# Order edges in a two-block model kernel, and a different end for its output projection

## The chip, the cores and the metric

The kernel runs on one core of one Trainium2 chip. The metric is the device time of one execution in microseconds (us). Three runs of the kernel before gave a median of 1876.63 us (1872.15 to 1878.21).

## What is computed

Four sequences of 256 tokens with 512 features (1024 tokens in all, float32) go through two blocks. Each step is x = x + f(layernorm(x)):

```python
x = x + L0_attn(ln(x))   # linear attention with a memory: sig_q @ M / (sig_q @ z), output projection
x = x + L0_ffn(ln(x))    # base matmul plus top-2 of 8 low-rank experts
x = x + L1_attn(ln(x))   # the mixer, below
x = x + L1_ffn(ln(x))    # base matmul plus top-1 of 4 low-rank experts
```

The mixer is a state-space layer. Its input projection gives, per token, a gate and x (8192 channels each), B and C (8 groups of 128 each) and dt (128 heads):

```python
x, B, C = silu(conv4(proj))                  # causal convolution over 4 tokens
dt = softplus(dt + dt_bias); A_dt = -exp(A_log) * dt
Y = (C B^T * exp(segsum(A_dt))) @ (x * dt) + (carry from the chunk before) + D * x
y = Y * rsqrt(mean(Y^2) + eps) * norm_w * silu(gate)
return y @ out_proj_w.T                      # 8192 -> 512
```

## The kernel before

The program is written once in order, and a scheduler then orders the instructions of every engine. It takes the written order as priority and its own estimates of time as readiness, so an instruction that looks ready can be placed ahead of one written earlier. Each engine then runs its own queue strictly in that order, and waits for semaphores where data or buffers come from another engine. `with tc.issue_after(ins):` adds an edge: each instruction of the block that runs on the same engine as `ins` is queued somewhere behind `ins`. It fixes no more than that, and it affects no other engine. The kernel keeps the instructions that edges refer to in `last`.

**First block (lines 198 to 350).** Eight token tiles of 128 are normalized (`layernorm`, L103 to L123: statistics on DVE, sqrt on ACT, `xn` on ACT or DVE, four transposes on PE, a copy to `xnT` on ACT). Eight heads follow in a pipeline (`queries`, `retrieve`, `turn`), then the output projection with weights `wo`, which POOL sums from four parts (L236 to L238), then the expert layer (`lora_mixture`, L146).

**Mixer (L353 to L992).** `time_steps` (L404) computes dt on all heads. It loads A_log and takes its exponential on ACT (L412). Then 72 units are worked through: 8 groups, each of one `bc` unit (its B and C channels) and 8 `pair` units (128 channels, that is two heads). A pair's unit has these stages:

- `stage_a` (L607) projects 1024 tokens to 256 channels (x and gate) with seven products of half-size blocks in place of eight (Strassen's scheme; token sums `tok`, weight sums `wsum` by POOL, L511 to L514). `project` (L517) issues them in four steps: each `product` is two 128x512 matmuls into PSUM banks `pd`, `pa`, `pb`; `keep` (L537, ACT) saves an intermediate value, and DVE adds at L549, L553 and L556 combine them. The instruction at L553 is `last["one"]`, the one at L556 `last["two"]`; the bank `pa` is used again by PE after L556 has read it. The weights of unit n+2 are loaded at the end of unit n.
- `stage_t` (L640), one unit later: transposes of xT (L683, into the only `mm2` bank pair), xdt and xdr (DVE, L686, L693), and the decay masks `cst`: loaded, 16 Relu (L705) and one Exp (L709) on ACT, multiplied with the group's `gt` on DVE (L711).
- `stage_c` (L716), two units later: 24 small matmuls `ps_y` (L725, L733), then on DVE y = D*x + ps_y (L741), on ACT the square (L743), on DVE y * norm_w * silu(gate) (L744) and the running sum of squares (L747).

The output projection is worked in as channel tiles become ready. Two tiles form one block i, and again seven products replace eight, for each half m of the 512 outputs. A product with number p covers two blocks (i-1, i) for one m; it is a PSUM bank `mm1` (two of them) that ACT copies to SBUF (L809) and POOL adds to `prod_d` in DRAM (L811). `begin_out` makes the token sums (L777) and queues seven products; a unit issues two of them after its first step and the rest after its third. POOL makes the weight sums (`out_weight_sums`, L763). Blocks 0 to 30 are done this way; channel tiles 62 and 63 are multiplied directly at the end.

**Order by hand.** In units 0 to 4 the dictionary `early` (L891) gives the stages that `turn` (L899) issues behind the last PE instruction, and `last["bar"]` holds all later products of `project` behind them. From unit 5 on `last["bar"]` is None. `last["pe"]` is the PE instruction written last.

**End.** Two further rounds of the loop (n = 72, 73) finish stages and products: block 30's fourteen products are added by DVE (L830) to what `load_prods` (L817) has loaded from `prod_d`. `put_together` (L832) combines seven products to four parts on DVE, for m = 0 and 1. The sum over channels for the norm is made by eight one-column matmuls (`ps_var`, L972). `finish(t)` (L979) puts two direct products and four transposed parts in one bank per token tile, adds to x (L992) and normalizes; the last expert layer follows, interleaved by `ready`.

Of the kernel before, what the change touches and what calls it, by code (L numbers as in the profile page):

```python
# [33 lines left out]
P = 128  # L34
# [19 lines left out]
def model_kernel(ctx: ExitStack, tc: tile.TileContext, a: dict, out: bass.AP):  # L54
# [25 lines left out]

    def toks(t):
        return slice(t * P, (t + 1) * P)
# [20 lines left out]
    def layernorm(t, psum, xnp, on_act=False):  # L103
# [19 lines left out]
        nc.scalar.copy(xnT[:, :, toks(t)], ps.rearrange("p (k t) -> p k t", k=KT))  # L123
# [74 lines left out]
    with ExitStack() as c0:  # L198
# [31 lines left out]
        for h in range(NKV):  # L230
# [7 lines left out]
            nc.gpsimd.tensor_tensor(wo[:, h, :], wo[:, h, :], s[:, 3, :], ALU.add)  # L238
# [114 lines left out]
    with ExitStack() as c1:  # L353
# [12 lines left out]
        last = {"pe": None, "one": None, "two": None, "adt": None, "bar": None}  # L366
# [37 lines left out]
        def time_steps():  # L404
# [7 lines left out]
            nc.scalar.activation(na, na, AF.Exp)  # L412
# [104 lines left out]
        def project(n, one, two):  # L517
# [17 lines left out]
            def keep(ps, i):  # L535
                c = snp.tile([P, 512], F32, tag=f"keep{i}", name=f"keep{n}_{i}")
                nc.scalar.copy(c, ps)  # L537
                return c
# [175 lines left out]
        ys = []  # L714

        def stage_c(n):  # L716
# [5 lines left out]
            for c in range(NT):  # L722
# [21 lines left out]
            nc.vector.scalar_tensor_tensor(  # L744
                y, y, normw[:, j : j + 1], hd["sg"], ALU.mult, ALU.mult
            )
            nc.vector.tensor_tensor(ssq, ssq, sq, ALU.add)  # L747
# [12 lines left out]

        osums, ysums = {}, {}

        def out_weight_sums(i):  # L763
            if 2 * i + 2 < NPAIR:
# [34 lines left out]
        def out_product(m, p, over, bank, to):  # L799

            ps = Psum.tile([P, 512], F32, bank, f"ps_p{over[-1]}_{m}_{p}")
# [3 lines left out]
            to(ps, m, p, over)  # L805

        def add_up(ps, m, p, over):
            st = osp.tile([P, 512], F32, tag="prod", name=f"prod{over[-1]}_{m}_{p}")
            nc.scalar.copy(st, ps)  # L809
            first = over[0] == 0  # L810
            nc.gpsimd.dma_start(  # L811
                out=prod_d[m][p // 2][p % 2], in_=st, accum_op=ALU.bypass if first else ALU.add
            )

        prods = []

        def load_prods():  # L817
            homes = [bcp.tile([P, 2, 512], F32, tag=f"tok{q}", name=f"out_a{q}") for q in range(3)]
            homes += [wsp.tile([P, 2, 512], F32, tag="wsum", name=f"out_b{q}") for q in range(2)]
            homes += [b2.tile([P, 2, 512], F32, tag="raw", name=f"out_c{q}") for q in range(2)]  # L820
            rest = homes[6]
            for m in range(2):
                tiles = homes[3 * m : 3 * m + 3]
                for q in range(3):
                    nc.sync.dma_start(out=tiles[q], in_=prod_d[m][q].rearrange("c p t -> p c t"))
                nc.sync.dma_start(out=rest[:, m], in_=prod_d[m][3][0])
                prods.append([tiles[p // 2][:, p % 2] for p in range(6)] + [rest[:, m]])

        def add_last(ps, m, p, over):
            nc.vector.tensor_tensor(prods[m][p], ps, prods[m][p], ALU.add)  # L830

        def put_together(m):  # L832

            g = prods[m]
            op = nc.vector.tensor_tensor
# [18 lines left out]
        def out_products(n, bank, to):  # L854
            for _ in range(min(n, len(todo))):
                m, p, over = todo.popleft()
                out_product(m, p, over, bank, to)
# [10 lines left out]
        next(steps)  # L868
        token_sums()
        for j in range(6):  # L870
            load_wout(j)
        for i in range(3):
            out_weight_sums(i)
# [14 lines left out]
        def first_sums(_):  # L888
# [7 lines left out]
            4: ([(stage_t, 2)], [(stage_c, 1)], [(stage_c, 2), (stage_t, 3)]),  # L896
        }

        def turn(n, i):  # L899

            if n not in early:
                step, m = [(None, 0), (stage_c, n - 2), (stage_t, n - 1)][i]
                if step and 0 <= m < len(units):
                    step(m)
# [7 lines left out]
        for n in range(len(units) + 2):  # L912
            a_steps = stage_a(n) if n < len(units) else iter(())
            bank, to = ("mm1", add_up) if n < len(units) else ("in", add_last)
            if n == len(units):
                load_prods()
# [147 lines left out]
```

## Time and profile before

| what | value |
|---|---|
| median of three runs | 1876.63 us |
| the profiled execution | 1876.13 us |
| its span in the profile | 1874.4 us |
| PE busy | 1804.8 us (96%) |
| DVE busy | 1366.1 us (73%) |
| ACT busy | 1166.4 us (62%) |
| POOL busy | 695.4 us (37%) |
| mean granted TensorE clock | 0.986 |
| mean DMA | 128 GB/s |

PE is TensorE's matmuls, PEld its weight loads, DVE the vector, ACT the scalar and POOL the GpSimd engine; SP issues DMAs. A share of busy time is an average over stages with different limits, so the views by stage and the waits of one engine say more than this table. A float32 matmul of 128x512 appears as two instructions in the trace and takes 0.857 us in all. The last instruction of the trace is the add at L194 of the last token tile and the store behind it.

### The profile page before, as it was taken

Reading aid. Unit: us, or ns where it says so; the run is one execution under the profiler, and the core shown is the slowest. Engines: PE = TensorE matmul, PEld = TensorE weight load, DVE = VectorE, ACT = ScalarE, POOL = GpSimd, SP = SyncE. Lnnn points to the kernel's source line nnn. Section 1 sums busy time; section 2 is a strip of 40 time slices with the busy share of each in tenths; the row PEclk is TensorE's granted clock in tenths of the full one; section 3 lists DMA queues with packets and bytes.
Section 4 is the critical chain, followed back from the end, with each engine's and each line's share of the span. In section 5 each row is a group of like instructions: output and inputs, shape, how many; then the busy total and the mean of one; then the engine's idle time right before and its main releaser. Section 6 shows DMA issues by size and latency. Waiting matters only on the chain.

```text
span 1874.4 us, 21313 instructions
## 1 busy us (share of the span) xinstructions
PE 1804.8 (96%) x7666; PEld 945.0 (50%) x7666; DVE 1366.1 (73%) x1495; ACT 1166.4 (62%) x2059; POOL 695.4 (37%) x681
## 2 busy tenths in 40 slices
PE   7999897999999999999999999999999999999988
PEld 4545544554554555455545454455454545455564
DVE  4433597888687868786878677887786887778871
ACT  3321238877577748775777676758775767766620
POOL 6311241335344533454235533543444344533100
PEclk9999998999999999999999999999999999999989
DMA  8100123345555555654555545554655555456701
GB/s 313 61 0 6 53 95 118 141 148 134 141 141 140 141 140 140 149 145 107 158 140 145 131 119 140 152 138 133 144 139 117 160 144 152 107 134 156 218 23 45
DMA packets 80329, 239.20 MB, mean 128 GB/s; under 512 B 9472, under 2 KB 10496, under 8 KB 70880
## 3 DMA queue, kind: packets, MB, share of 16 engines
q1 hardware_dynamic: 48768, 171.49, 25.8%
q0 software_dynamic: 30880, 65.30, 21.5%
q8 instruction: 61, 1.00, 0.2%
q10 hardware_dynamic: 576, 1.05, 0.2%
q14 instruction: 44, 0.36, 0.1%
HBM read 177.78 MB, written 60.03 MB: 127 GB/s over the span
## 4 chain that ended last, share of the span: by engine, by line
PE 63%; ACT 14%; DVE 14%; DMA 5%; issue 4%; POOL 0%; SPq 0%; DVEq 0%; ACTq 0%; POOLq 0%
PE pa L526 17%; PE ps_p L804 12%; PE pd L526 8%; ACT cst L709 4%; ACT cst L705 4%; PE ps_y L725 4%; PE pb L526 4%; DMA cst<-cs_d 4%; PE f_pso L172 3%; PE ps_o L307 3%; PE ps_q L95 3%; DVE xT L569 3%; DVE cst L711 2%; PE ps_xt L683 2%; PE ps_y L733 2%
## 5 line engine op out<-in xcount | busy, mean ns | idle before, releaser
L811 POOL DMA_DIRECT2D prod_d<-prod x210 | 178.0, 927 | 524.8 <-ACT prod L809 509.9
L705 ACT ACTIVATE cst<-cst,cs 128x128 f32<-128x128 f32 x1024 | 326.7, 395 | 31.4 <-DMA cst<-cs_d 31.0
L711 DVE TENSOR_TENSOR cst<-cst,gt 128x1536 f32<-128x1536 f32 x128 | 232.7, 1842 | 113.9 <-ACT cst L709 113.8
L569 DVE SCALAR_TENSOR_TENSOR xT<-raw,convw,xT 128x1020 f32<-128x1020 f32 (+2 forms) x216 | 300.9, 1394 | 1.6
L511 POOL TENSOR_TENSOR wsum<-win 128x256 f32<-128x256 f32 x72 | 94.1, 1307 | 354.5 <-DMA win<-in_win 198.7
L743 ACT ACTIVATE xdt<-xT 128x1024 f32<-128x1024 f32 x64 | 67.7, 1058 | 253.1 <-DVE xT L741 253.1
L709 ACT ACTIVATE cst<-cst 128x3072 f32<-128x3072 f32 x64 | 176.9, 2764 | 0.7
L804 PE MATMUL ps_p<-xT,wout 128*128 128x512 f32 x372 | 172.2, 595 | 1.4 <-DVE xT L744 1.4
L725 PE MATMUL ps_y<-cst,xdt 128*64 128x128 f32 x2048 | 161.1, 276 | 0.1
L526 PE MATMUL pa<-xnT,wsum 128*128 128x512 f32 x288 | 144.6, 625 | 9.0 <-ACT keep L537 8.9
L526 PE MATMUL pa<-tok,win 128*128 128x512 f32 x288 | 137.4, 600 | 12.2 <-DVE sg L556 12.1
L725 PEld LDWEIGHTS ps_y<-cst,xdt 128*64 128x64 f32 x2048 | 120.0, 137 | 52.7 <-issue 49.2
L526 PE MATMUL pd<-tok,wsum 128*128 128x512 f32 x288 | 139.0, 604 | 6.5 <-POOL wsum L511 4.5
L526 PE MATMUL pa<-xnT,win 128*128 128x512 f32 x288 | 136.8, 596 | 0.0
L526 PE MATMUL pa<-tok,wsum 128*128 128x512 f32 x288 | 135.8, 593 | 0.8 <-ACT keep L537 0.8
L549 DVE TENSOR_TENSOR raw<-pb,keep 128x512 f32<-128x512 f32 x72 | 49.4, 686 | 118.4 <-PE pb L526 118.1
L526 PE MATMUL pd<-xnT,wsum 128*128 128x512 f32 x288 | 135.6, 592 | 0.1
L526 PE MATMUL pb<-xnT,win 128*128 128x512 f32 x288 | 135.6, 592 | 0.0
L809 ACT COPY prod<-ps_p 128x512 f32<-128x512 f32 x210 | 117.7, 575 | 25.6 <-PE ps_p L804 21.3
L804 PEld LDWEIGHTS ps_p<-xT,wout 128*128 128x128 f32 x372 | 70.0, 190 | 88.2 <-issue 84.3
L804 PE MATMUL ps_p<-ysum,osum 128*128 128x512 f32 x248 | 112.1, 593 | 0.0
L537 ACT COPY keep<-pa 128x512 f32<-128x512 f32 x144 | 83.0, 577 | 38.6 <-PE pa L526 38.5
(217 smaller groups left out, 3178.3 us busy)
## 6 DMA issues: line engine op xcount, KB each, us to landing
cst<-cs_d SPq DMA_DIRECT2D x64, 1536.0 KB, 6.3
prod_d<-prod POOLq DMA_DIRECT2D x210, 256.0 KB, 4.3
win<-in_win SPq DMA_DIRECT2D x144, 256.0 KB, 3.9
wout<-in_wout SPq DMA_DIRECT2D x64, 256.0 KB, 4.1
wo_s<-in_wo POOLq DMA_DIRECT2D x8, 1024.0 KB, 5.9
wq<-in_wq SPq DMA_DIRECT2D x8, 256.0 KB, 3.7
x_d<-x SPq DMA_DIRECT2D x8, 256.0 KB, 2.0
xr<-x_d SPq DMA_DIRECT2D x2, 1024.0 KB, 7.4
```

What stands on the lines that cost most here:

```text
L511: op(v[:, 0], w[:, 1, 0:2], w[:, 1, 2:4], ALU.add)
L526: last["pe"] = nc.tensor.matmul(ps, lhsT=wt[:, k, :], rhs=tk[:, k, :], start=start and k == 0, stop=k == 1, skip_group_check=not start,)
L537: nc.scalar.copy(c, ps)
L569: nc.vector.scalar_tensor_tensor(d[:, :, k:], src[:, :, : SEQ - k], convw[:, i, TAPS - 1 - k : TAPS - k], d[:, :, k:], ALU.mult, ALU.add,)
L705: nc.scalar.activation(m[:, hh, c, :], m[:, hh, c, :], AF.Relu, bias=cs[:, c, h : h + 1], scale=1.0)
L709: nc.scalar.activation(mf, mf, AF.Exp, scale=-1.0)
L711: nc.vector.tensor_tensor(mf[:, hh], mf[:, hh], gr.rearrange("p c l -> p (c l)"), ALU.mult)
L725: last["pe"] = nc.tensor.matmul(flat(py)[e, toks(c)], lhsT=xdt[:, c, e], rhs=m[:, hh, c, :], start=True, stop=c % 2 == 0,)
L743: nc.scalar.activation(sq, y, AF.Square)
L804: last["pe"] = nc.tensor.matmul(ps, lhsT=w, rhs=y, start=i == over[0], stop=i == over[-1])
L809: nc.scalar.copy(st, ps)
L811: nc.gpsimd.dma_start(out=prod_d[m][p // 2][p % 2], in_=st, accum_op=ALU.bypass if first else ALU.add)
```

## The change

It has these parts:

1. The exponential of A_log is queued behind the last copy to `xnT` on ACT (`marks["xnT"]`), and the first three weight sums of the output projection behind the last sum of `wo` on POOL (`marks["wo"]`). Unit 0's products are queued behind the matmuls of dt on PE.
2. `early` gets entries for units 5 and 6, so that `last["bar"]` stays in force up to unit 6.
3. The last two DVE instructions of `stage_c` become `stage_d`, queued on DVE behind `last["two"]`. The ACT copies of the products of a unit's first step are queued behind the unit's last `keep`; the copies of its third step come after all its products (`add_up` works off the list `taken`).
4. Seven-product blocks end at block 29 (`SEVEN` is 30). The last four channel tiles (60 to 63) are multiplied directly, eight token tiles times four. Four token tiles begin early: with tiles 60 and 61 before the last `stage_c`, with tile 62 behind it. The loop has no rounds 72 and 73; the last seven products of block 29 (m = 0) go through DRAM like the others and are loaded again by `load_prods(0)`. `put_together(1)` runs on POOL, `put_together(0)` on DVE.

```diff
-        nc.scalar.copy(xnT[:, :, toks(t)], ps.rearrange("p (k t) -> p k t", k=KT))
+        marks["xnT"] = nc.scalar.copy(xnT[:, :, toks(t)], ps.rearrange("p (k t) -> p k t", k=KT))
...
-            nc.scalar.activation(na, na, AF.Exp)
+            with issue_after(marks["xnT"]):
+                nc.scalar.activation(na, na, AF.Exp)
...
-            nc.vector.scalar_tensor_tensor(
-                y, y, normw[:, j : j + 1], hd["sg"], ALU.mult, ALU.mult
-            )
-            nc.vector.tensor_tensor(ssq, ssq, sq, ALU.add)
+            outputs[n] = y, sq, hd["sg"]
+
+        def stage_d(n):
+            if n not in outputs:
+                return
+            j, (y, sq, sg) = units[n][1], outputs.pop(n)
+            with issue_after(last["two"]):
+                nc.vector.scalar_tensor_tensor(y, y, normw[:, j : j + 1], sg, ALU.mult, ALU.mult)
+                nc.vector.tensor_tensor(ssq, ssq, sq, ALU.add)
             ys.append(y)
...
         next(steps)
+        last["bar"] = last["pe"]
         token_sums()
         for j in range(6):
             load_wout(j)
-        for i in range(3):
-            out_weight_sums(i)
+        with issue_after(marks["wo"]):
+            for i in range(3):
+                out_weight_sums(i)
...
-            4: ([(stage_t, 2)], [(stage_c, 1)], [(stage_c, 2), (stage_t, 3)]),
+            4: ([(stage_t, 2)], [(stage_c, 1), (stage_d, 1)], [(stage_c, 2), (stage_d, 2), (stage_t, 3)]),
+            5: ([], [(stage_c, 3)], [(stage_d, 3), (stage_t, 4)]),
+            6: ([], [(stage_c, 4)], [(stage_d, 4), (stage_t, 5)]),
...
-            out_products(2, bank, to)
+            next(a_steps)
+            out_products(2)
             turn(n, 0)
-            next(a_steps, None)
+            next(a_steps)
+            with issue_after(last["keep"]):
+                add_up()
             turn(n, 1)
-            next(a_steps, None)
-            out_products(share - 2, bank, to)
+            next(a_steps)
+            out_products(share - 2)
+            add_up()
...
+        last["two"] = None
+        load_prods(1)
+        for p in ORDER:
+            out_product(0, p, (SEVEN - 1,))
+            add_up()
+        N = len(units)
+        with issue_after(last["pe"]):
+            stage_c(N - 2)
+            stage_d(N - 2)
+            stage_t(N - 1)
+        load_prods(0)
...
+        parts = {1: put_together(1)}
+        AHEAD = 4
+        with issue_after(last["pe"]):
+            for t in range(AHEAD):
+                for j in (NPAIR - 4, NPAIR - 3):
+                    out_project(t, j, "mm1" if t < 2 else "in")
+        with issue_after(last["pe"]):
+            stage_c(N - 1)
+            stage_d(N - 1)
+        with issue_after(last["pe"]):
+            for t in range(AHEAD):
+                out_project(t, NPAIR - 2)
+        pv = Psum.tile([P, 2, 512], F32, "mm2", "ps_var")
+        with issue_after(last["pe"]):
+            for t in range(NT):
+                last["pe"] = nc.tensor.matmul(
+                    pv[:, 0, t : t + 1], lhsT=ssq[:, toks(t)], rhs=ones, start=True, stop=True
+                )
...
+        parts[0] = put_together(0)
...
-            for j in (NPAIR - 2, NPAIR - 1):
-                nc.tensor.matmul(
-                    ps, lhsT=ys[j][:, toks(t)], rhs=wouts[j], start=j == NPAIR - 2, stop=j == NPAIR - 1
-                )
+            for j in [NPAIR - 1] if t < AHEAD else range(NPAIR - 4, NPAIR):
+                with issue_after(last["pe"]):
+                    out_project(t, j)
+            ps = outs.pop(t)
```

## The prediction

> **What bounds the kernel now.** The busy times by stage come first: each row is a stretch of the span, then the busy time of PE, PEld, DVE, ACT and POOL, the granted TensorE clock, and the DMA.
>
> ```profile
> 0.00:215.00 215.00, 192.69 (x696) 105.99 (x696) 92.41 (x250) 56.00 (x93) 59.17 (x67) 0.98 0.26 93
> 215.00:360.00 145.00, 130.97 (x536) 69.12 (x537) 120.30 (x109) 89.87 (x152) 43.07 (x40) 0.93 0.29 105
> 360.00:1760.00 1400.00, 1378.77 (x5993) 709.58 (x5992) 1092.06 (x1020) 992.32 (x1768) 591.10 (x574) 1.00 0.55 140
> 1760.00:1875.00 115.00, 102.39 (x444) 60.32 (x442) 61.31 (x119) 28.19 (x48) 2.09 (x3) 0.92 0.22 63
> ```
>
> PE is the bound everywhere: 1804.8 of 1874.4 us. An order of issue can only win PE's idle time (22, 14, 21 and 13 us in the four stages) and the work done at a low clock. So I list the waits of PE, then its timeline at the longest ones; the bracket is the idle time before an instruction and what ended it.
>
> ```profile
> 22.80 1.12 PE L122 MATMUL ln_ps<-ident,xn 128*128 128x128 f32 x4 [4.54 <-ACT xn L117]
> ...
> 328.16 3.75 PE L526 MATMUL pd<-tok,wsum 128*128 128x512 f32 x4 [3.70 <-POOL wsum L511]
> ...
> 574.46 1.98 PE L526 MATMUL pa<-tok,win 128*128 128x512 f32 x4 [1.34 <-DVE sg L556]
> ...
> 1791.14 3.58 PE L972 MATMUL ps_var<-ones,ssq 128*128 128x1 f32 x16 [4.92 <-DVE ssq L747]
> ```
>
> Within 360 to 1760 the list of waits has three entries only: DVE sg L556 9.3 us in 8 times, ACT keep L537 8.9 us in 8, DVE xT L741 2.9 us in 5.
>
> **First block.** ACT's timeline shows why PE stood at 22.8:
>
> ```profile
> 21.73 0.31 ACT L412 ACTIVATE per_head<-per_head 128x128 f32<-128x128 f32 x1 [5.17 <-DMA per_head<-in_A_log]
> 21.95 0.80 ACT L117 ACTIVATE xn<-x,ln_sh,ln_rs 128x512 f32<-128x512 f32 x1
> ```
>
> The Exp of A_log waits for its load, and the last token tile's xn stands behind it. The edge sends the Exp behind the last xnT copy (214.3), where ACT is idle for 12.24 us and where the result is not read until L450 at 252.3. Won: 4.54 us, and the clock, granted at 0.64 from 22.8 to 30.0 (7.2 x 0.36 = 2.6): 7.1. What is late next: the tile's shift is ready at 16.26; xn 0.81, transposes 0.44 and copy 0.57 end at 18.1, just where PE stopped (18.3). Added: the table load of 1.28 that hid in this wait now stands before head 0's first Exp; ps_n of that head waited only 0.27, so between 0 and 1.28 shows, and I take 0.6, since ps_q of the next head covers some. On POOL the osum sums of two blocks (8 x 0.72) go behind the last wo sum (66 us); their reader is at 317, and POOL has nothing then until 111.8: nothing. Net -6.5 (bounds -3 and -7.1, the weak end if the later wq loads fall behind).
>
> **First seven units.** At 328.16 unit 6's first product stood in PE's queue before unit 5's rest; its weights could be loaded only when unit 4's last product ended (322), so 3.70 and, before it, 1.39 us were idle, and about 2.3 us went to a clock of 0.74 and 0.53 over 322 to 332. Edges for units 5 and 6 forbid that order: -7.4. They also forbid what filled 309 to 315: unit 5's pa, pb and pa, while stage_c(2) waited for the masks' products L711 (313.3). PE will stand there: L711 can end between 311.1 (the Exp's end at 307.6 plus 2 x 1.75) and 313.3, so 2.0 to 4.2, and L741 adds 1.3 before the transposes: 3.3 to 5.5, with 0 to 3.4 of cold clock. ps_dt before unit 0's first product (215.66, run in 1.8 us before wdt was used) is between -0.3 and +1. Net between -4.4 and +2.5; I take -2.5, nearer the gain because the longest wait in the trace is the one removed.
>
> **Each pair.** The DVE queue at 574:
>
> ```profile
> 571.38 1.28 DVE L744 SCALAR_TENSOR_TENSOR xT<-xT,normw,sg 128x1024 f32<-128x1024 f32 x1
> 572.58 1.22 DVE L747 TENSOR_TENSOR ssq<-ssq,xdt 128x1024 f32<-128x1024 f32 x1
> 573.72 0.68 DVE L556 TENSOR_TENSOR sg<-pa,keep 128x512 f32<-128x512 f32 x1
> ```
>
> L744 and L747 are stage_d; the edge puts them behind L556. L556 then ends at 572.0, before PE is through with pd (573.1): the 1.34 goes, and no other wait takes its place. That is 9.3 us over 8 places; I take 8.5. Where no wait shows (L556 at 377.96, L744 at 380.23) the order is this already. Readers of y come later by 0.68 us; the next product is 3.4 us further on.
>
> The 210 copies L809 (0.57 each) go behind keep. Cover: at 394.70 keep ends, two copies end at 395.8, and the product that wants their bank starts at 398.11, 2.3 us later. In the 8 places where keep is late (2.08 us at 636.4), two copies stood ahead of it, 1.1 us; but there a product already ran in front (633.18), which now waits for the copies. So between 0 and 1.1 a place is won; I take 1.5 in all. POOL's writes of prod move with the copies by up to 5 us; behind them stand the weight sums, due a unit (21 us) later, and the osum sums: nothing. If that cover is gone it is the second rival. Net -10 (bounds -14 and, without the rival, 0).
>
> **Tail.** Removed: the 4.92 before ps_var, and the cold clock after it, 0.50 over 1791.1 to 1798 and 0.81 to 1802 (3.4 + 0.8): 9.1. Now four products with channel tile 62 (4 x 0.857 = 3.43) lie over the chain L741, L744, L747 (3.6); 0.3 stays, 1.5 if two other DVE adds get in between as now; I take 0.7: -8.4. Products: 21 closing ones become 7, 16 direct ones become 32: two more, +1.7. The part transposes are the same.
>
> New wait: the last unit's transposes (ps_xt) follow stage_c of the unit before at once, and all eight direct products stand behind them by an edge. In the trace 8.8 us of products lay between (1766.87 to 1775.65). PE will be there at 1760.5 + 7 x 0.857 + 2.75 = 1769.3. They need L741 (1.28) and the Silu of the last xT, which ended at 1771.0 on an ACT without a gap since 1757.5, and ACT now gets seven copies (4.0) that DVE did as L830. So 1.7 to 5.7; I take 3, since DVE loses fourteen L830 and four L777 and the conv ends earlier. The price of such a wait at the clock: the Trainium skill (TensorE: Matmul & The Clock Gate, HAM oscillation) says idle gaps above about 3.4 us make the clock fall. The rows put it lower: after 2.81 us (269.3) the clock was 0.66 over the next 5 us, after 2.85 us (1828.4) 0.59 over 7, after 2.08 and 1.34 it stayed 1.00. By the rule my 3 us cost nothing more; by the rows up to 3.4. I follow the rows at half, 1.7: +4.7.
>
> The products' return through DRAM: last one 1766.5, copy 0.6, issue 0.9, landing 4.4, load 4.6, seven DVE adds 4.2: 1781.7, against a first use near 1788. Cover 6 us, also for the loads queued on SP in front. put_together(1) on POOL: seven adds of 128x512 at 1.27 (row L236) from 1769 to 1778, due at 1788. Here the skill speaks against the change (SBUF — State Buffer, Who interferes with whom): a DVE operation with two SBUF inputs and a GpSimd one exclude each other, the later blocks whole; that would be up to 7 x 1.27 = 8.9 us of DVE. The row: L777 took 0.68 alone and 1.21 beside POOL sums (558.13), 0.53 more, so 3.7 for seven. I take the row; on PE's path it is inside the 3 us above. By the rule the tail would end 4 later. Unchanged: the last layernorm's wait of 2.85 and its cold clock, 2.9. Net -2 (bounds -6 and +4).
>
> **Sum.** -6.5 - 2.5 - 10 - 2 = -21. The profiled execution took 1876.13 us (span 1874.4, 1.7 around it): 1855.1. It lies 0.5 under the median of the three runs, 1876.63, so 1855.5.
>
> **Rivals.** (a) The edges of the units do not do what they say: an edge fixes a place on one engine, and the rest of the order is chosen anew, so that the small waits of units and tail come back elsewhere and only the A_log fix counts: 1876.6 - 6.5 = 1870. For it: 21 us of idle time in 72 units is already little, and the remaining waits have three different releasers. Against it: L556's eight waits have one cause each time. Its low variant, in which only the tail pays back, lies near 1864.
> (b) Slower: copies behind keep starve the two product banks. Place: the third product of a unit. It decides when the copies end over 2.3 us after keep, that is, when ACT puts a table load and an Exp (1.28 + 2.76 = 4.0) between. The first bank is then free at 394.7 + 4.0 + 0.6 = 399.3, 1.2 us after 398.11; in half of the 60 units with products that is 36 us, and 1855 + 36 = 1891. For it: the Exp follows keep closely, at 370.9 and 373.4. Against it: there the product starts at 377.09, after the Exp's end at 376.1 plus a copy.
> (c) Nothing: the stall at 309 gets its cold clock, the tail takes its bad end (+2.5, +4), the pairs give nothing: 1876.6 - 6.5 + 6.5 = 1877.
>
> **How the numbers follow.** Forecast 0.54 (1840 to 1865), (a) 0.20, (b) 0.17, (c) 0.09. 0.3% is 5.6 us, about what a measurement of this kernel can tell from no change. Faster: 0.54 + 0.20 = 0.74; same 0.09; slower 0.17. The range takes the good bounds of first block, units and pairs in part, 1838, and reaches to 1883, over (a) and (c) and the mild end of (b): about 0.17 is left out.
>
> **What would show it.** Right: no idle time before ln_ps at 22.8 and clock 1.00 in the slice 20 to 40; PE waits on DVE sg L556 under 2 us within the pairs; the two waits at 323 and 328 gone, one of 2 to 6 us at stage_c(2); no wait of 4.9 at ps_var, one at the last ps_xt. Wrong: PE waiting for ACT prod copies over 10 us in all, waits for keep grown, or finish(0) waiting for put_together.

## Result and profile after

The changed kernel takes 1883.49 us (median, 1877.42 to 1890.73) beside 1875.3 of the kernel before on the same chip: ratio 1.0044, 95% interval 1.0031 to 1.0056, some 8 us slower. 1855.5 was forecast. The profiled execution has a span of 1880.9 us (before: 1874.4). Lines of the changed kernel have moved: `keep` is L540, the add that frees `pa` L559, Relu of the masks L708, their product with `gt` L714, y L744, stage_d L754 and L755, the copies of products L822.

Busy time by stage again (PE, PEld, DVE, ACT, POOL, clock, DMA):

```profile
0.00:215.00 215.00, 195.93 (x737) 110.92 (x738) 95.01 (x252) 57.55 (x94) 65.22 (x73) 0.98 0.26 94
215.00:360.00 145.00, 132.23 (x545) 68.31 (x545) 125.64 (x116) 104.03 (x180) 45.64 (x39) 0.99 0.32 111
360.00:1760.00 1400.00, 1373.11 (x5957) 705.58 (x5954) 1051.46 (x1014) 958.85 (x1737) 539.22 (x568) 1.00 0.54 140
1760.00:1885.00 125.00, 105.23 (x438) 61.06 (x436) 44.75 (x89) 25.50 (x41) 11.45 (x12) 0.89 0.25 72
```

The first two stages improved: PE gets more work done, and the clock in the second is 0.99, not 0.93. In the third PE is busy for 5.7 us less than before in the same 1400 us; 3.9 of that is the first wait of the end, at 1755.9, which already falls into this window. The last stage is longer, at a lower clock.

Read along the trace by when PE ends the last projection product of a unit, the changed kernel is ahead by 8.2 us at unit 0, by 13.6 at unit 6 and unit 9, and by 10.3 at unit 71 (1750.3 against 1760.7). So the pairs, forecast at -10, gave 3.3 back. From there to the end it takes 130.6 us, not 113.7: 16.9 lost where -2 was forecast.

PE's waits in the pairs (us in total, times, longest; 345 to 1750):

```profile
PE ps_xt L686 <- DVE xT L744: 10.8, 7, 1.9
PE pa L529 <- ACT keep L540: 9.4, 19, 1.8
PE pa L529 <- DVE sg L559: 2.4, 5, 0.5
```

The wait on the add fell from 9.3 to 2.4, as forecast. But the wait for y (xT) before the transposes rose from 2.9 to 10.8, and keep is waited for 19 times, not 8. Behind both, ACT's waits for the load of the masks rose (the kernel before, then the changed one):

```profile
ACT cst L705 <- DMA cst<-cs_d: 25.4, 20, 3.5
```

```profile
ACT cst L708 <- DMA cst<-cs_d: 69.3, 37, 4.0
```

No wait of PE for a product's copy appears in this stretch, so the second rival, which had the right sign, did not happen.

PE's long waits in the first units and at the end:

```profile
299.76 0.40 PE L728 MATMUL ps_y<-cst,xdt 128*64 128x128 f32 x2 [3.92 <-DVE cst L714]
...
1755.90 2.08 PE L813 MATMUL ps_p<-xT,osum 128*128 128x512 f32 x2 [3.87 <-ACT prod L822]
...
1766.37 2.07 PE L813 MATMUL ps_p<-ysum,wout 128*128 128x512 f32 x2 [3.42 <-ACT prod L822]
...
1775.18 1.63 PE L686 MATMUL ps_xt<-ident,xT 128*128 128x128 f32 x8 [2.13 <-DVE xT L744]
...
1793.27 1.92 PE L1015 MATMUL ps_var<-ones,ssq 128*128 128x1 f32 x16 [2.04 <-DVE ssq L755]
```

4.54 at 22.8 and the pair of waits at 323 and 328 are gone; the one at stage_c(2) came as forecast (3.92 and 1.17). At the end the wait before ps_var fell from 4.92 to 2.04, and two new ones stand ahead of it: products that wait for a free bank, whose copy waits for one of only three staging buffers, each held until its write has landed. DVE, too, stood still there for 15.9 us; that row comes with the runs on the new end.

### The profile page after: what moved, and what is told of

It is laid out like the page before. It is cut to its first block, busy times and chain, and to the rows that moved or that the text cites. A ratio compares the mean times of both kernels' runs of the same rounds, so it can differ in the third digit from the quotient of the medians.

```text
span 1880.9 us, 21210 instructions
## 1 busy us (share of the span) xinstructions
PE 1806.5 (96%) x7670; PEld 945.9 (50%) x7670; DVE 1316.9 (70%) x1470; ACT 1145.9 (61%) x2051; POOL 661.5 (35%) x691
## 4 chain that ended last, share of the span: by engine, by line
PE 53%; ACT 20%; DMA 13%; DVE 7%; issue 3%; POOL 2%; SPq 0%; DVEq 0%; POOLq 0%; ACTq 0%
PE pa L529 13%; PE ps_p L813 9%; DMA cst<-cs_d 9%; ACT cst L708 8%; PE pd L529 7%; ACT cst L712 4%; PE ps_y L728 3%; PE pb L529 3%; PE f_pso L174 3%; DMA prod_d<-prod 3%; PE ps_q L97 3%; PE ps_o L309 3%; DVE cst L714 2%; ACT L712 2%; ACT keep L540 2%
## 5 line engine op out<-in xcount | busy, mean ns | idle before, releaser
L823 POOL DMA_DIRECT2D prod_d<-prod x217 | 189.8, 959 | 555.0 <-ACT prod L822 535.8
L708 ACT ACTIVATE cst<-cst,cs 128x128 f32<-128x128 f32 x1024 | 323.6, 393 | 78.5 <-DMA cst<-cs_d 78.5
L714 DVE TENSOR_TENSOR cst<-cst,gt 128x1536 f32<-128x1536 f32 x128 | 227.3, 1800 | 131.8 <-ACT cst L712 127.8
L572 DVE SCALAR_TENSOR_TENSOR xT<-raw,convw,xT 128x1020 f32<-128x1020 f32 (+2 forms) x216 | 285.3, 1322 | 2.2
L514 POOL TENSOR_TENSOR wsum<-win 128x256 f32<-128x256 f32 x72 | 98.9, 1374 | 336.9 <-DMA win<-in_win 259.5
L813 PE MATMUL ps_p<-xT,wout 128*128 128x512 f32 x360 | 165.0, 593 | 0.4 <-ACT prod L822 0.4
L822 ACT COPY prod<-ps_p 128x512 f32<-128x512 f32 x217 | 118.8, 586 | 24.6 <-DMA prod_d<-prod 21.5
L540 ACT COPY keep<-pa 128x512 f32<-128x512 f32 x144 | 82.2, 570 | 49.7 <-PE pa L529 49.7
```

What stands on the lines that cost most here:

```text
L514: op(v[:, 0], w[:, 1, 0:2], w[:, 1, 2:4], ALU.add)
L540: last["keep"] = nc.scalar.copy(c, ps)
L572: nc.vector.scalar_tensor_tensor(d[:, :, k:], src[:, :, : SEQ - k], convw[:, i, TAPS - 1 - k : TAPS - k], d[:, :, k:], ALU.mult, ALU.add,)
L708: nc.scalar.activation(m[:, hh, c, :], m[:, hh, c, :], AF.Relu, bias=cs[:, c, h : h + 1], scale=1.0)
L714: nc.vector.tensor_tensor(mf[:, hh], mf[:, hh], gr.rearrange("p c l -> p (c l)"), ALU.mult)
L813: last["pe"] = nc.tensor.matmul(ps, lhsT=w, rhs=y, start=i == over[0], stop=i == over[-1])
```

## Experiments

The theory after the result: the copies behind keep cost the pairs through their transfers, and the new end costs the rest; the edges are harmless. The rival: edges reshuffle all queues, and no part can be blamed. "Early copies" means that a unit's first two products are copied at once, as before (in e3, e6 and e12 the later products too; in e10 and e14 these are copied after all products of the unit, as in the changed kernel). e1 to e4, e5 to e8, e9 to e12 and e13 to e15 each shared a chip, on which the kernel before took 1876.66, 1875.42, 1873.61 and 1872.65 us; across these groups the ratios are the safer comparison.

### One part at a time

`e1_first_only` is the kernel before plus part 1's first edge:

```diff
-            nc.scalar.activation(na, na, AF.Exp)
+            with issue_after(marks["xnT"]):
+                nc.scalar.activation(na, na, AF.Exp)
```

> The kernel before, with only the exponential of A_log queued behind the last xnT copy. Theory (the loss sits in the new end, and in the copies behind keep; the first block wins what was forecast): -7.0 us, 1868, ratio 0.996; PE has no idle time before the last ln_ps at 22.8, and everything later is as before, moved by 7. Rival (the gain is only borrowed: the loads and sums of the first block fall behind and the time is given back by the start of the mixer): -2 or less, ratio 0.999 or more.

`e2_no_tail` has all of parts 1 to 3, and the old end; `work_off` stands there for the changed kernel's `add_up`. `e3_no_tail_early` is the same, but each product is copied as soon as it is issued, as in the kernel before:

```diff
-            (to or (lambda *q: taken.append(q)))(ps, m, p, over)
+            to(ps, m, p, over)
...
-            with issue_after(last["keep"]):
-                work_off()
...
-            work_off()
```

> The kernel before with parts 1 to 3 of the change (all edges, the copies behind keep among them); its own end with blocks 0 to 30 in seven products, the adds of the last products by DVE, and the last sums free of an edge. Theory (the end lost 17 us, the pairs gave back 3 of what the first units had won): the end of unit 71 comes 10 us earlier, as in the changed kernel, and the end takes 114 us as before, so -10, 1865, ratio 0.9945 (0.993 to 0.996). Rival (the order of the whole is chosen anew with each edit and the loss cannot be tied to a part; or the slow pairs come from the edges and grow): ratio 0.999 or more.

> As the kernel with parts 1 to 3 and the old end, but the copies of a unit's first two products are issued at once, as before, not behind keep. Theory (the deferred copies start their writes of 256 KB together with the load of the 1.5 MB of decay masks, which then lands 2 us later, and ACT waits for it): the masks land in 6.3 us at the median again, not 8.1; ACT's waits for them within 345 to 1750 fall from 69 to about 30 us; PE's new waits for xT and keep (some 9 us more than before) go; against the version with the copies behind keep 4 to 10 us faster, ratio to the kernel before 0.990 to 0.993. Rival 1 (the loss in the pairs comes from stage_d behind the last add, which moves the conv of the next unit and so y): no difference between the two, 0.9945 for both. Rival 2 (copies behind keep do gain, since keep no longer stands behind two copies): slower than with them by 1 to 4 us.

`e4_tail_only` is the kernel before plus part 4.

> The kernel before with part 4 alone (the last four channel tiles multiplied directly, four token tiles begun ahead, the last seven products through DRAM), no edge of parts 1 to 3. Theory: the time from the last projection product to the end grows from 114 to about 130 us, of it 7 us of PE waiting for copies of products that wait for staging buffers, and about as much again in cold clock: +10 to +17, 1887 to 1893, ratio 1.005 to 1.009. Rival (the new end is hurt only by what the edges of part 3 leave late, such as the copies and the masks of the last unit): within 4 us of before, ratio 0.998 to 1.002.

| kernel | median us | ratio to before | 95% interval |
|---|---|---|---|
| A_log edge only (e1) | 1864.37 | 0.9933 | 0.9915 to 0.9951 |
| parts 1 to 3, old end (e2) | 1872.76 | 0.9976 | 0.9961 to 0.9991 |
| the same, early copies (e3) | 1862.71 | 0.9930 | 0.9913 to 0.9948 |
| part 4 only (e4) | 1888.94 | 1.0068 | 1.0048 to 1.0089 |
| before, same chip | 1876.66 | | |

From these: A_log edge -12.3; the other edges, those of units 5 and 6 and of stage_d among them (e3 less e1) -1.7; copies behind keep (e2 less e3) +10.1; new end (e4) +12.3. The first three are steps on one way, from before to e2 (-3.9 in all), so the test is whether e2 and e4 add up: they give +8.4, and 1.0044 of 1876.66 is +8.3. They do, so the rival that no part can be blamed is out.

e3 came within its range, and e1 gained more than the 7 us expected. e2 lies between its theory and its rival: in its trace the lead falls from 11.7 us at unit 9 to 8.7 at unit 71, and the end takes 116.2 us, not 114. e4 took the time that was expected, but not for the reason given: PE waited in its end 3.0 us for copies, where 7 were expected, and 8.7 for y.

### What the copies behind keep collide with

Landing times first (KB, median us from issue to landing), e3 and then e2:

```profile
cst<-cs_d SPq DMA_DIRECT2D x58, 1536.0 KB, 6.7
prod_d<-prod POOLq DMA_DIRECT2D x205, 256.0 KB, 5.0
```

```profile
cst<-cs_d SPq DMA_DIRECT2D x58, 1536.0 KB, 8.0
prod_d<-prod POOLq DMA_DIRECT2D x203, 256.0 KB, 6.1
```

And one unit's writes and mask load in time, e3 and then e2:

```profile
662.32 1.75 POOL L821 DMA_DIRECT2D prod_d<-prod  x2
...
667.28 0.33 SPq L637 DMA_DIRECT2D cst<-cs_d  x1
```

```profile
665.34 2.07 POOL L828 DMA_DIRECT2D prod_d<-prod  x2 [3.88 <-ACT prod L826]
...
668.46 0.33 SPq L637 DMA_DIRECT2D cst<-cs_d  x1
```

In this unit the two writes start 5.0 us ahead of the load of the masks with early copies, and 3.1 ahead behind keep, where they are still in flight when it starts. Over all 58 loads of the stretch: a load that had writes beside it for under 0.5 us landed in 6.2 us at the median in e3 and 6.3 in e2; one that had them for over 2 us took 7.8 and 8.2. With early copies 31 of the 58 loads are of this second kind, behind keep 50. To see whether this is the cost, the same two kernels ran without the writes:

```diff
-            first = over[0] == 0
-            nc.gpsimd.dma_start(..., in_=st, accum_op=ALU.bypass if first else ALU.add)
+            if over[0] == 0:
+                nc.gpsimd.dma_start(out=prod_d[m][p // 2][p % 2], in_=st)
```

The queues of PE, DVE and ACT have the same order with and without the writes, so the pairs differ in the transfers alone (with POOL's time to issue them, and the time for which a write holds its staging buffer).

> The kernel with parts 1 to 3 and the old end, copies of the products behind keep, but without their writes: only the first block of each half is still written to DRAM, the sums of the later blocks are left out (the copies to SBUF stay, the output lacks these products). With its partner below it measures whether the 10 us that the copies behind keep cost go through DMA. Theory (the writes, started late and together, collide with the load of the masks): without writes the masks land in under 6.5 us at the median (8.0 with them), ACT waits under 35 us for them within 345 to 1750 (69.6 with them), and the time is within 2 us of the partner, near 1860. Rival (the place of the copies in ACT's queue is what costs, by holding masks, keep and PSUM banks): still 7 us or more slower than the partner, ACT's waits for the masks unchanged.

> The partner: the copies of a unit's first two products at once, and the same writes left out (the sums of the later blocks are missing in the output). Theory: the masks land in about 6 us, and the time is at most 4 us below the version with writes (1862.7), since with early copies the writes lie where nothing waits for them: 1859 to 1863, equal to the late version. Rival (ACT's queue): equal to its version with writes, 7 us or more faster than the late one.

| copies | with writes | without | the writes cost |
|---|---|---|---|
| behind keep | 1872.76 (e2) | 1841.20 (e5, ratio 0.9808, 0.9793 to 0.9823) | 31.6 |
| at once | 1862.71 (e3) | 1854.32 (e6, ratio 0.9877, 0.9860 to 0.9894) | 8.4 |

Neither expectation held in full. The theory had the two equal without writes; in fact the order behind keep is then 13.1 us better, so it is a good order by itself. It loses because it exposes 31.6 us of transfers where the other exposes 8.4. ACT's waits for the masks and PE's for keep and y tell the same. First two of ACT's rows of e2, then PE's rows of e2, then one of ACT's rows and the only PE row of e5 (us in total, times, longest; 345 to 1730):

```profile
ACT cst L708 <- DMA cst<-cs_d: 69.6, 37, 4.3
...
ACT prod L826 <- DMA prod_d<-prod: 11.7, 6, 3.2
```

```profile
PE pa L529 <- ACT keep L540: 13.4, 19, 1.9
PE ps_xt L686 <- DVE xT L744: 9.1, 7, 1.9
PE pa L529 <- DVE sg L559: 1.4, 3, 0.5
```

```profile
ACT cst L708 <- DMA cst<-cs_d: 8.6, 20, 2.0
```

```profile
PE ps_xt L686 <- DVE xT L744: 0.8, 3, 0.3
```

Without the writes ACT waits 8.6 us for the masks, not 69.6, and PE 0.8, not 23.9. So the cost goes through the transfers. How much of it goes through the masks, and how much through copies that wait for a staging buffer (the second row of e2), these runs do not separate: leaving out the writes takes both away. The Trainium skill (DMA: Bandwidth & Descriptors, Queues, rings and completion order) says that a DMA engine takes turns between the queues that have work for it. The landing times agree: writes issued by POOL and the load issued by SP go through different queues and still slow each other; without the writes the load lands in 6.2 us (e5) and 6.3 (e6).

### Masks in two transfers

```diff
-            nc.sync.dma_start(out=cst..., in_=cs_d[2 * j : 2 * j + 2, :]...)
+            for hh in range(2):
+                nc.sync.dma_start(out=cst[:, hh : hh + 1]..., in_=cs_d[2 * j + hh : 2 * j + hh + 1, :]...)
```

> Parts 1 to 3 with the old end and the copies behind keep, but the load of the masks is two transfers of 768 KB, one for each head, in place of one of 1536 KB, so that ACT can begin on the first head's masks when half has landed. Theory (what the collision costs goes through the wait of ACT for the masks): ACT's waits for the masks within 345 to 1730 fall from 69.6 us to under 25, PE's waits for keep and xT from 22.5 to under 10, 6 to 12 us faster than without the split (1872.8), ratio 0.991 to 0.995. Rival (the cost goes another way: staging buffers held by slow writes, weight loads landing later): within 3 us of 1872.8, ratio 0.996 to 0.999.

> The same split of the masks' load, with copies at once. Theory: with early copies ACT waits only 29 us for the masks, half of it before idle time of no consequence: 0 to 5 us faster than without the split (1862.7), ratio 0.990 to 0.993. Rival (twice as many transfers on SP and in the queues cost more than the early start brings): slower than 1862.7 by 2 us or more.

Behind keep: 1857.38 (0.9924, 0.9903 to 0.9945), ACT's waits for the masks 27.9 us instead of 69.6. The ratio is in the theory's range, and the waits just miss it (under 25); 10 us (ratios) to 15 (medians) of the 31.6 come back. With early copies: 1842.87 (0.9837, 0.9820 to 0.9854), ACT's waits 14.3 instead of 29.0: 17 us (ratios) to 20 (medians) faster than unsplit, where 0 to 5 were expected. The scheduler also ordered ACT, DVE and PE anew in both, so how much of this is the earlier landing alone is not shown.

### The new end, taken apart

`e7_stage7` puts copies 4 to 6 of the last seven products into the three buffers of keep; `e8_tail_dve` drops the return through DRAM; `e9_stage7_order` is e7 with one more edge; `e10_best2` is e8 with that edge and early copies.

```diff
 e7:  -                st = osp.tile([P, 512], F32, tag="prod", ...)
      +                st = (snp if tag else osp).tile([P, 512], F32, tag=tag or "prod", ...)
 e8:  +        load_prods(0)          # before the last seven products
      ...
      -            add_up()
      +            nc.vector.tensor_tensor(prods[0][p], ps, prods[0][p], ALU.add)
 e9:  +        with issue_after(last["masks"]):     # L714 of unit 71
                   parts[0] = put_together(0)
```

> The changed kernel, but copies 4 to 6 of the last seven products go to the three buffers of keep, free by then, so that six staging buffers stand where three did; all else as in the changed kernel. Theory (in the new end PE waits for banks whose copies wait for a staging buffer until its write has landed): the waits of PE for copies of products in the end (7.7 us) fall under 1, the clock is granted at over 0.9 from 1755 to 1772, and the end takes 117 to 123 us instead of 131: -8 to -13, near 1872, ratio to the kernel before 0.996 to 0.999. Rival (the wait only moves: the transposes of the last unit, the DRAM return or put_together is late next): the waits for copies go, one for ps_xt or ps_out of as many us takes their place, and the time stays within 3 us of 1883, ratio 1.002 or more.

> The changed kernel, but the last seven products do not return through DRAM: both halves are loaded from prod_d before them, they go to the other PSUM banks, and DVE adds each to the loaded value, as in the kernel before. Theory (the return through DRAM with its staging buffers is the step that failed): no waits for copies of products in the end, 12 to 15 us less than the changed kernel, near 1870, ratio 0.994 to 0.998; a wait of 2 to 4 us before the last ps_xt stays, since DVE now has seven adds before y. Rival (the new end is slow for its serial chain stage_c, transposes, stage_c with all products ahead of it): a wait of 6 us or more before the last ps_xt and the time within 5 us of 1883.

> The changed kernel with six staging buffers for the last seven products, and with one edge more: put_together(0), whose first add waits on DVE for the products' return from DRAM, is queued behind the masks' products L714 of unit 71, so that it no longer stands in DVE's queue ahead of y of unit 70 (L744), for which the last transposes wait. Theory (the wait of 9.1 us before the last ps_xt in the run with six buffers is this queue place, a load that heads the queue): the wait before ps_xt falls under 2.5 us, the end takes 117 to 121 us, -6 to -10 against six buffers alone, near 1875, ratio 0.998 to 1.001. Rival (the return itself is too late, wherever it is queued: finish(0) or y of unit 71 behind the adds waits as long): a wait of 5 us or more before ps_var or ps_out takes its place, time within 3 us of 1883.

> The changed kernel with three things put otherwise: copies of a unit's first two products at once (not behind keep), the last seven products added by DVE from PSUM to what was loaded (no return through DRAM), and put_together(0) queued behind the masks' products L714 of unit 71. Theory (the new end, freed of its two blocked queues, is worth no more than the old one: -3.5 at ps_var, +1.7 for two more matmuls, +1.5 to 3 at ps_xt and the banks of the last products): as the version with parts 1 to 3, early copies and the old end (1862.7) within 4 us, ratio 0.991 to 0.995. Rival 1 (as forecast, the end begun ahead is a gain once its returns are off the path): 1857 or less, ratio under 0.990. Rival 2 (POOL's put_together(1) beside DVE's adds slows both, and the waits before the last products and ps_xt stay as long as in the run without the edge, 7 us in all): 1867 to 1871, ratio 0.995 to 0.997.

e7: 1883.74 (1.0043, 1.0027 to 1.0060), no gain; the theory's size fell. PE's waits for copies went down from 7.7 to 2.6 us, and this took their place (DVE first, then PE):

```profile
1780.75 0.69 DVE L845 TENSOR_TENSOR out<-out 128x512 f32<-128x512 f32 x1 [17.98 <-DMA out<-prod_d]
1781.36 1.27 DVE L744 SCALAR_TENSOR_TENSOR xT<-xT,dd,ps_y 128x1024 f32<-128x1024 f32 x1
```

```profile
1782.69 1.97 PE L686 MATMUL ps_xt<-ident,xT 128*128 128x128 f32 x8 [9.13 <-DVE xT L744]
```

L845 is the first add of put_together(0). It stood in DVE's queue ahead of y of unit 70, and waited for the products' return from DRAM; DVE was idle for 18 us, y behind it, and PE behind y. In the changed kernel the same add stood at the same place; there PE's waits for copies held PE back as well, so that only 2.13 us showed before ps_xt:

```profile
1769.65 4.28 DVE L845 TENSOR_TENSOR out<-out 128x512 f32<-128x512 f32 x1 [15.89 <-DMA out<-prod_d]
```

e9 puts it further back: the wait for y falls from 9.13 to 1.38, but 2.96 and 0.91 come back before unit 71's stage_c, and the time is 1879.37 (1.0045, 1.0025 to 1.0065): no gain by the ratio, where 6 to 10 us were expected. Without the return (e8): 1874.87 (0.9990, 0.9977 to 1.0004), some 9 us better than the changed kernel, where 12 to 15 were expected. With everything repaired (e10): 1863.08 (0.9950, 0.9933 to 0.9966), no better than the old end with the same copies (e3, 0.9930).

The last group prices what is left: e14 the new end, e13 and e15 the edges.

> All edges, early copies, the masks in two transfers, and the new end repaired (DVE adds the last products from PSUM, put_together(0) queued behind the masks' products): beside the same with the old end (1842.9) it prices the new end by itself, free of staging, return and late masks. Theory (the stretch from the last projection product to ps_var is a serial chain of 30 us in every version, not bound by PE, so that PE's work there is free: the old end has 21 matmuls of closing products there and 16 direct ones behind ps_var, the new one 19 and 20): four matmuls more behind ps_var, +3.4, and the last layernorm's wait +0.6: 1844 to 1850. Rival (the new end begun ahead is a gain of 3 or more once repaired): 1840 or less.

> The kernel with only the A_log exponential moved, its writes left out as in the two runs without writes (the sums of the later blocks are missing in the output). Beside the version with all edges, early copies and no writes (1854.3) it prices the edges of the first units and of stage_d apart from any collision of transfers. Theory (these edges trade waits on the add L559 for waits on y and keep, and are worth next to nothing of the 11 us forecast): 1852 to 1857, within 3 us. Rival (they are worth the forecast and the writes eat it): 1860 us or more.

> The kernel before with only the A_log exponential moved and the masks in two transfers; none of the other edges. Beside all edges with the split (1842.9) it says whether those edges gain once the masks land sooner. Theory (the edges are worth little): within 4 us of 1842.9. Rival (with the masks in time the edges of stage_d and the units give the 11 us that were forecast): 1850 or more.

e14, the repaired end on the split kernel, took 1851.07 (0.9897, 0.9881 to 0.9914), 1 us above the range expected: 8.2 slower than the old end there (e12; 11 by the ratios). In the two traces the end is 6.5 longer. Where it goes, from each trace (us):

| kernel | last projection product to ps_var | ps_var to the last layernorm on PE | from there to the end | in all |
|---|---|---|---|---|
| before | 30.5 | 37.3 | 46.0 | 113.7 |
| changed | 43.0 | 40.0 | 47.7 | 130.6 |
| six buffers (e7) | 41.1 | 38.6 | 47.3 | 127.0 |
| and the edge (e9) | 35.8 | 41.6 | 47.7 | 125.1 |
| no return (e8) | 33.5 | 40.0 | 47.7 | 121.1 |
| repaired, split (e14) | 30.6 | 41.6 | 47.6 | 119.8 |
| old end, split (e12) | 30.1 | 36.9 | 46.3 | 113.3 |

The first column is the point. It is 30 to 31 us in every kernel whose end is not blocked, because DVE, not PE, bounds it: in this stretch DVE is busy for 30.0 of 30.4 us in the kernel before and for 29.6 of 30.1 in e12 (PE: 25.4 and 25.2). PE's work there costs nothing. In the changed kernel DVE has only 23.7 us of work in the stretch and stands idle for 19.1, of them 15.9 before L845. The old end has 21 matmuls of 0.857 us in it, the new one only 19 (7 closing ones and 12 ahead), and leaves 20 behind ps_var where the old one leaves 16. Four matmuls are 3.4 us of the 4.7 in the second column; 0.6 is the last layernorm's wait, 3.47 for 2.85. The third column follows the clock: the stretch at 0.50 behind that wait lasts 6.83 us in the two kernels with 46.0 and 46.3, and 10.24 in the others. The old end can have either (e15: 10.24 us, and 48.0 in this column), so this column is no cost of the new end.

The new end also gave DVE less to do, so why is the first column not shorter? POOL. In e14 (DVE, then POOL) and in e12 (DVE) the same operations:

```profile
1740.83 2.75 DVE L715 TENSOR_TENSOR cst<-cst,gt 128x1536 f32<-128x1536 f32 x1
1743.50 2.28 DVE L755 SCALAR_TENSOR_TENSOR xT<-xT,normw,sg 128x1024 f32<-128x1024 f32 x1
1745.70 2.28 DVE L756 TENSOR_TENSOR ssq<-ssq,xdt 128x1024 f32<-128x1024 f32 x1
```

```profile
1742.04 2.66 POOL L849 TENSOR_TENSOR out<-out,out 128x512 f32<-128x512 f32 x1
```

```profile
1740.60 1.75 DVE L715 TENSOR_TENSOR cst<-cst,gt 128x1536 f32<-128x1536 f32 x1
...
1743.47 1.27 DVE L757 SCALAR_TENSOR_TENSOR xT<-xT,normw,sg 128x1024 f32<-128x1024 f32 x1
...
1745.27 1.22 DVE L758 TENSOR_TENSOR ssq<-ssq,xdt 128x1024 f32<-128x1024 f32 x1
```

Beside put_together(1) on POOL they take 1.0 to 1.1 us more each; with another L715 (2.49) and an add (1.25 for 0.68) that is 4.4 us on DVE, nearly what its seven adds of 0.68 would have cost there. No run puts these adds back on DVE, so this is a reading of one trace.

e13 and e15 price the edges: without writes 1856.46 (0.9915, 0.9899 to 0.9931) for the A_log edge alone against 1854.32 with all edges; with the split 1842.19 (0.9847, 0.9827 to 0.9866) against 1842.87. In the traces unit 71 ends within 0.3 us for the first two. So by medians and traces they are worth 2 us or less. The ratios of the pair without writes are 0.4% apart; these two ran on different chips, and 7 us can't be excluded.

## Why the prediction was wrong

**First block (-6.5): right.** e1's trace gains 8.1 by the end of unit 0, with the wait of 4.54 and its cold clock gone as worked out. In the fifteen traces with this edge the gain at that point is 3.6 to 10.1, with a median of 6.9. The rest of e1's -12.3 was not forecast, and lies where the change orders nothing: 2.8 more come by unit 6 (e1 keeps the waits of the first units, 2.51, 3.64, 1.67, 1.39 and 3.70, but the clock over 215 to 360 is 0.98 and not 0.93), and in this trace, the fastest of e1's six executions, 4.6 in the pairs. e4, without the edge, wins 2.8 there too. Why is not shown.

**First units (-2.5) and stage_d (-8.5): the waits went as forecast, and the time did not.** The two waits at 323 and 328 turned into 3.92 and 1.17 at stage_c(2), inside the 3.3 to 5.5 that was worked out. Waits on the add L559 went from 9.9 (e1) to 4.9 (e3), but those for y from 2.0 to 4.6: y and the transposes are next in line. "No other wait takes its place" was the error; all these edges together measured -1.7, with some 5 us either way.

**Copies behind keep (-1.5): the first step that failed.** The prediction counted what ACT and PE do at each place, and of the moved DMAs it said: "POOL's writes of prod move with the copies by up to 5 us; behind them stand the weight sums [...] and the osum sums: nothing." It asked what is queued behind them, and not which transfer they run beside. That transfer is the load of the masks, 1.5 MB a unit. Measured +10.1: 13.1 of a gain that was also undersized, and 23.2 more for the writes.

**Tail (-2): the second step that failed.** Three terms of it.

- "Removed: the 4.92 before ps_var [...] -8.4" took the wait for time that matmuls would fill. The stretch has its length from DVE, 30 us with the old end and with the repaired one, and the change takes two matmuls out of it and puts four behind it: +4.7 in the second column. The wait itself was mis-sized as well: 2.04 stayed, where 0.7 was taken. The chain L741, L744, L747 was put at 3.6 us, but L744 writes over the y that the square on ACT still reads. In the changed kernel DVE stood idle for 1.12 us for it, and the chain took 4.8.
- "The products' return through DRAM [...] Cover 6 us" compared the return with the use in finish(0). Its first reader, L845, stood in DVE's queue ahead of y and kept DVE idle for 15.9 us; and the staging buffers (three, each held until the write landed) were not counted at all. The first column rose by 12.5 us. (The terms given there add up to 1781.2, not 1781.7.)
- The wait at ps_xt was named, at 3 us for another reason (Silu); it was 2.13 in the changed kernel and 9.13 once the copies no longer hid it.

The repairs do not add up one by one: more buffers, and more buffers with the edge, gained nothing that the ratios show; only dropping the return did.

**Rivals.** (a) predicted that units and pairs give nothing, which is what the edges gave. (b) had the sign and the wrong mechanism. How much the repaired end still costs stays open: e10 less e3 is 0.4 us by medians and 3.8 by ratios, e14 less e12 is 8.2 and 11; by the traces' ends it is 4.2 and 6.5. In none of these is it a gain.

**Beyond both kernels.** The A_log edge with split masks and the old end (e15, 1842.19, ratio 0.9847; e12 the same within the interval) is 1.5% faster than the kernel before and 2.0% faster than the changed one (0.9847 / 1.0044).

## What to carry to other kernels

When an instruction that issues a transfer is moved, ask which other transfer is in flight at the new time, and who waits for that one; the queue behind it is only half the answer. Before filling a wait of the bounding engine, measure how long the stretch around it is and which engine sets that: where another engine sets it, work put there is free, and work taken out comes back elsewhere. An operation that waits for a load should stand behind everything in its queue that others need now.

## What the runs showed of the hardware

The clock after a short wait depends on more than the wait. In all seventeen traces the granted clock is either 1.00 or 0.50, never between, and in each trace it changes only at multiples of 3.41 us from one starting point: every stretch at 0.50 within the kernel lasts 3.41, 6.83 or 10.24 us. A mean such as 0.64 or 0.74 is a mixture of the two. So it matters how a wait falls into these steps. A wait of 3.43 us of the kernel before put 2.40 of it into one step, and the clock fell at the step's end; one of 3.64 in e1 was shared by two steps, 1.85 and 1.79, and the clock stayed (step, PE busy, clock, DMA):

```profile
280.56:283.97 3.41, 1.01 (x7) 1.00 0.91 386
283.97:287.38 3.41, 2.38 (x9) 0.50 0.20 82
```

```profile
270.34:273.75 3.41, 1.56 (x11) 1.00 0.96 393
273.75:277.16 3.41, 1.62 (x10) 1.00 0.20 82
277.16:280.57 3.41, 3.41 (x9) 1.00 0.00 0
```

e7 and e9 have the same wait before ps_var, 1.39 and 1.38 us, with the same matmuls around it. The rows below are the 5 us around it and the 5 behind, e7 and then e9.

```profile
1798.00:1803.00 5.00, 3.61 (x21) 1.00 0.52 194
1803.00:1808.00 5.00, 5.00 (x29) 1.00 0.00 2
```

```profile
1785.00:1790.00 5.00, 3.62 (x20) 0.94 0.49 188
1790.00:1795.00 5.00, 5.00 (x13) 0.50 0.00 2
```

In both the step with the wait holds 2.0 us of matmuls; in e9 1.45 of them are the one-column ones of ps_var, in e7 0.62. The fall costs e9 3 us that the edge had won. The Trainium skill (TensorE: Matmul & The Clock Gate, Part 1) has the gate look at a window of about 3.4 us that runs on its own, and the steps agree with that; that one-column matmuls count for less than others would explain e9, but no run tests it. These rows speak against the prediction, which priced a wait by its length, by the page's threshold and by its own rows alike. A stretch at 0.50 costs at most half its length, 1.7 to 5.1 us here by estimate from the three lengths; a sum should carry each such term as a range from nothing up.

Of the DVE operations in e14, those with both inputs in SBUF grew by 0.6 to 1.1 us beside POOL's adds, while L690, which reads PSUM, kept 1.21; POOL's own adds grew from 1.27 to as much as 2.66. That is what the skill (SBUF — State Buffer, Who interferes with whom) says of which operations collide, and by its lock the later of two would wait for the other to end, here up to 1.27 us. The changed kernel shows more: its L845 took 4.28 us, where the same add took 0.69 in e7, beside three of POOL's adds and two of the DMAs that it issues.
